# Left blocks of split products read from their first place, and their combinations made in the row buffers

## The chip, the cores and the metric

The kernel runs on one core of one Trainium2 chip. The metric is the device time of one execution in microseconds. The time before is the median of three runs. All profiles are single executions, taken by the hardware profiler.

The core has engines with queues of their own: TensorE (PE in the profile, its weight loads PEld), VectorE (DVE), ScalarE (ACT), GpSimd (POOL) and SyncE (SP). Transfers are issued from the queues of SyncE, ScalarE and GpSimd.

## The reference

Two graph layers over 4096 nodes with 512 features, each with a residual and a layer norm. The second layer is attention over the adjacency matrix:

```python
# layer 0
x = layernorm(x + relu(adj @ (max(sign(x), 0) @ sign(W0).T)))
# layer 1
node_att = softmax(x @ node_w, axis=0)
h = x @ edge_w
e = where(adj > 0, h @ h.T, -9e15)
combined = node_att * softmax(e, axis=1)
out = layernorm(x + (adj * combined) @ (x @ weight) + bias)
```

All data are 32-bit floats. Here only the last large product matters, the aggregation `(adj * combined) @ (x @ weight)`, which the kernel computes as `((adj * combined) @ x) @ weight`, transposed.

## The kernel before

The kernel works in stages: layer 0 (to about 507 us), the projection `h` (to 606), the scores `e` with their row statistics (to about 1086 us), and the aggregation with the final layer norm (to the end). Products are done with seven multiplications for eight (Strassen's scheme in Winograd's form): two operands of 2 x 2 blocks each are combined by additions into seven left and seven right operands, and the seven products are added up.

**The left operands** of the aggregation are seven combinations of blocks of `x` after layer 0. They are made there once and stored in DRAM, `lop_d`, in one piece for each of four groups of rows:

```python
    lop_d = [dram.tile([P, 7, BG, HD], F32, name=f"lop_d{g}") for g in range(HG)]

    lop2_d = [dram.tile([P, len(SPLIT), 7, BG // 2, P], F32, name=f"lop2_d{g}") for g in range(HG)]
...
def left(b, low, high):

    to = lop_d[b // BG][:, :, b % BG, :]
    l11, l21, l12, l22 = low[:, :HD], low[:, HD:], high[:, :HD], high[:, HD:]
    s4, s1, s2, s3 = (sums_l[:, n, :] for n in range(4))
    nc.vector.tensor_sub(s3, l11, l21)
    nc.vector.tensor_add(s1, l22, l21)
    nc.vector.tensor_sub(s2, s1, l11)
    nc.vector.tensor_sub(s4, l12, s2)
    nc.gpsimd.dma_start(to[:, 0, :], l11)
    nc.gpsimd.dma_start(to[:, 1:4:2, :], high.rearrange("p (h f) -> p h f", h=2))
    nc.gpsimd.dma_start(to[:, 2, :], s4)
    nc.gpsimd.dma_start(to[:, 4:, :], sums_l[:, 1:, :])
```

**The aggregation** is 16 blocks, four column groups `g` times four row groups `r`. Each block is seven products `m`. Its right operands are made by VectorE and ScalarE during the block before (L823 to L856: scores shifted, exponential, times adjacency, then four differences); its left operands are loaded from `lop_d[r][:, m]`, 512 KB each, into a pool of four buffers:

```python
    rows = ctx.enter_context(tc.tile_pool(name="rows", bufs=4))
...
    lopp = ctx.enter_context(tc.tile_pool(name="lopp", bufs=4))
```

From the fifth block to the last but one, three of the seven products (`SPLIT = 6, 4, 3`) are themselves split into seven smaller ones. Their seven left blocks (three raw quarters of the left operand, `l11`, `l12` and `l22`, and four combinations, into which `l21` goes too) are made once, while the first column group (`g` = 0) still does these products whole. `order` says in which sequence the products come:

```python
def order(self, two):


    ends = (1, 2) if self.r % 2 else (2, 1)
    if self.last:
        order = 1, 0, 5, 2, 6, 4, 3
    elif two:
        order = ends[0], 6, 5, 4, 0, 3, ends[1]
    else:
        order = ends[0], 0, 4, 6, 5, 3, ends[1]
    for m in order:
        if two and m in SPLIT:
            for ns in ((1, 2), (6,), (0, 5), (3, 4)):
                yield Sums(self, m, ns=ns)
        else:

            more = bool(self.r) and m == order[0]
            keep = self.r < HG - 1 and m == order[-1]
            for h in range(2):
                yield Sums(self, m, h, more, keep)
```

`lefts` runs at the end of a whole product of the first column group. In the order of the program it takes a buffer of the left pool for the combinations, makes them with four VectorE additions, and at the next step stores raw quarters and combinations, seven blocks in all, to `lop2_d` from the scalar queue. `main` runs a block and calls it:

```python
def lefts(self, m, lop):

    (l11, l21), (l12, l22) = [[lop[:, k : k + 2, f : f + P] for f in (0, P)] for k in (0, BG // 2)]
    s = lopp.tile([P, 4, BG // 2, P], F32, name="left2", tag="lop")
    s4, s3, s2, s1 = (s[:, n] for n in range(4))

    tc.keep_in_program_order(nc.vector.tensor_add(s1, l21, l22))
    tc.keep_in_program_order(nc.vector.tensor_sub(s2, s1, l11))
    tc.keep_in_program_order(nc.vector.tensor_sub(s3, l11, l21))
    tc.keep_in_program_order(nc.vector.tensor_sub(s4, l12, s2))
    to = lop2_d[self.r][:, SPLIT.index(m)]
    yield
    nc.scalar.dma_start(to[:, :2].rearrange("p n b f -> p (n b) f"), lop[:, :, :P])
    nc.scalar.dma_start(to[:, 2:6], s)
    nc.scalar.dma_start(to[:, 6], l22)
...
def main(self, between, two):
    uses = deque(u for u in plan if u.unit is self)
    whole = sum(u.work for u in uses)
    halves = (None for m in [u.m for u in uses if u.ns and u.ns[0] == 1] for _ in self.second(m))
    stores = deque()
    past = 0
    while plan and plan[0].unit is self:
        u = plan.popleft()
        u.seed()
        u.multiply()
        evict()
        written.append(u)
        for ahead in list(plan)[:3]:
            ahead.seed()
        past += u.work
        if stores:
            next(stores.popleft(), None)
        if not u.ns:
            next(halves, None)
        if u.end:
            free.append(self.right(u.m))
            if not self.g and u.m in SPLIT:
                stores.append(self.lefts(u.m, lops["lop"]))
                next(stores[0])
        between(past / whole, u.work)
    if stores:
        next(stores.popleft(), None)
```

A product then loads what it needs and multiplies. For a whole product that is one transfer; for a split one two, the first four blocks into one buffer and the last three into another:

```python
def multiply(self):
    r, m = self.unit.r, self.m
    if self.begin and not self.ns:
        lops["lop"] = lopp.tile([P, BG, HD], F32, name="lop")
        nc.sync.dma_start(lops["lop"], lop_d[r][:, m])
    elif self.begin:
        for n, c in (("low", slice(0, 4)), ("high", slice(4, 7))):
            lops[n] = lopp.tile([P, 4, BG // 2, P], F32, name="lop2", tag="lop")
            nc.sync.dma_start(lops[n][:, : c.stop - c.start], lop2_d[r][:, SPLIT.index(m), c])
    if self.ns:
        products = []
        for k, n in enumerate(self.ns):
            at = self.lefts[n]
            lop = lops["high"][:, at - 4] if at > 3 else lops["low"][:, at]
            products.append((self.bank[:, ts(k, W // 2)], lop, self.unit.halves[n], BG // 2))
    else:
        products = [(self.bank, lops["lop"][:, :, ts(self.h, P)], self.unit.right(m), BG)]
    start = not r and self.w == W
    for ps, lop, rop, K in products:
        for k in range(K):
            nc.tensor.matmul(ps, lop[:, k, :], rop[:, k, :], start=start, stop=(k == K - 1), skip_group_check=True)
            start = False
```

Each product of 128 x 512 in 32-bit floats shows as two records of TensorE, so a whole product `m` is 2 halves x 4 matmuls x 2 = 16 records.

**The row buffers** (`rows`, four of 2 KB a partition) hold rows of `x` and other short-lived things in earlier stages. In the aggregation only the finishing step of a column group uses them, for the residual rows:

```python
def load(self, some=range(BG)):
    rows_ = x1_d[self.A * W : (self.A + 1) * W, :]
    if self.last:
        xb = take()
        nc.gpsimd.dma_start(xb, rows_.rearrange("(b p) d -> p b d", p=P))
        self.xbs = [xb[:, i, :] for i in range(BG)]
        return
    for i in some:
        self.xbs[i] = rows.tile([P, D], F32, name="xb1", tag="rows")
        nc.sync.dma_start(self.xbs[i], rows_[ts(i, P), :])
```

The first finishing step follows the fourth block (the last of column group 0). Its loads are in the sync queue, as the left loads are[...].

Of the kernel before, what the change touches and what calls it, by code (L numbers as in the profile page):

```python
# [11 lines left out]
F32 = mybir.dt.float32  # L12
# [6 lines left out]
P = 128  # L19
# [5 lines left out]
SPLIT = 6, 4, 3  # L25
# [4 lines left out]
def kernel(  # L30
# [13 lines left out]
    nc = tc.nc  # L44
# [5 lines left out]
    BG = W // P  # L50
    HB = NB // 2
    HG = NG // 2
# [5 lines left out]
    rows = ctx.enter_context(tc.tile_pool(name="rows", bufs=4))  # L58
    small = ctx.enter_context(tc.tile_pool(name="small", bufs=2))
    dram = ctx.enter_context(tc.tile_pool(name="dram", bufs=1, space=bass.MemoryType.DRAM))  # L60
# [17 lines left out]

    lop_d = [dram.tile([P, 7, BG, HD], F32, name=f"lop_d{g}") for g in range(HG)]

    lop2_d = [dram.tile([P, len(SPLIT), 7, BG // 2, P], F32, name=f"lop2_d{g}") for g in range(HG)]

# [5 lines left out]
    def seven(lop, rop, dests, after):  # L90
# [43 lines left out]
        def m3(ps, q, c11, c12, c21, c22):  # L134
            nc.vector.tensor_add(c12, c12, ps)
            after(q, 1)

        multiply(0, 0, True, m1)
        multiply(1, 5, True, u2)
        multiply(2, 4, True, nothing)  # L140
        multiply(1, 6, False, u3)
        multiply(0, 1, False, m2)
# [16 lines left out]
    with (  # L159
# [184 lines left out]
        with tc.manual_schedule(engines={mybir.EngineType.DVE, mybir.EngineType.Activation}):  # L344
            for n in range(NB):
                b = n // 2 + n % 2 * HB
# [43 lines left out]
        lops = stream.tile([P, 4, HK, HD], F32, name="lops", tag="stream")  # L390
        l11, l12 = we_s[:, :HK, :HD], we_s[:, HK:, :HD]
        l21, l22 = we_s[:, :HK, HD:], we_s[:, HK:, HD:]
        s4, s1, s2, s3 = (lops[:, n] for n in range(4))
# [59 lines left out]
    lopp = ctx.enter_context(tc.tile_pool(name="lopp", bufs=4))  # L453
# [345 lines left out]
    class Aggregate:  # L799
# [149 lines left out]
        def lefts(self, m, lop):  # L949

            (l11, l21), (l12, l22) = [[lop[:, k : k + 2, f : f + P] for f in (0, P)] for k in (0, BG // 2)]
            s = lopp.tile([P, 4, BG // 2, P], F32, name="left2", tag="lop")
            s4, s3, s2, s1 = (s[:, n] for n in range(4))

            tc.keep_in_program_order(nc.vector.tensor_add(s1, l21, l22))
            tc.keep_in_program_order(nc.vector.tensor_sub(s2, s1, l11))
            tc.keep_in_program_order(nc.vector.tensor_sub(s3, l11, l21))
            tc.keep_in_program_order(nc.vector.tensor_sub(s4, l12, s2))
            to = lop2_d[self.r][:, SPLIT.index(m)]
            yield  # L960
            nc.scalar.dma_start(to[:, :2].rearrange("p n b f -> p (n b) f"), lop[:, :, :P])
            nc.scalar.dma_start(to[:, 2:6], s)
            nc.scalar.dma_start(to[:, 6], l22)

        def right(self, m):
            r11, t1, r21, r22 = self.q
# [36 lines left out]
    lops = {}  # L1003
# [5 lines left out]
    class Sums:  # L1009
# [32 lines left out]
# [3 lines that stand above are left out]
                lops["lop"] = lopp.tile([P, BG, HD], F32, name="lop")  # L1045
                nc.sync.dma_start(lops["lop"], lop_d[r][:, m])
            elif self.begin:
                for n, c in (("low", slice(0, 4)), ("high", slice(4, 7))):
                    lops[n] = lopp.tile([P, 4, BG // 2, P], F32, name="lop2", tag="lop")
                    nc.sync.dma_start(lops[n][:, : c.stop - c.start], lop2_d[r][:, SPLIT.index(m), c])  # L1050
            if self.ns:
                products = []
                for k, n in enumerate(self.ns):
# [10 lines that stand above are left out]
            if self.keep:  # L1064
                kept.append(self.bank)
# [371 lines left out]
```

## Time and profile before

| | before |
|---|---|
| time, median of 3 runs | 1962.94 us |
| single runs | 1972.32, 1954.82, 1962.94 us |
| span of the profiled run | 1966.4 us |
| TensorE busy | 98% |
| VectorE busy | 71% |
| ScalarE busy | 52% |
| GpSimd busy | 15% |
| mean granted clock of TensorE | 0.993 |
| moved by transfers | 521.82 MB, 265 GB/s |

A line of the page's groups reads: line of the kernel, engine, operation, output and inputs, shape, count; then busy time in all and the mean of one in ns; then the engine's idle time just before these instructions and what ended most of it. `lop_d` in a group stands for both DRAM tensors of left operands, since numbers in names are left out. The issues of transfers, with size of one and the median time from issue to landing, are these for the stores and loads concerned (from 980 us on):

```profile
lop<-lop_d SPq DMA_DIRECT2D x112, 512.0 KB, 4.8
...
lop<-lop_d SPq DMA_DIRECT2D x33, 384.0 KB, 5.0
...
lop_d<-left ACTq DMA_DIRECT2D x12, 512.0 KB, 5.9
...
lop_d<-lop ACTq DMA_DIRECT2D x12, 256.0 KB, 5.2
...
lop_d<-lop ACTq DMA_DIRECT2D x12, 128.0 KB, 5.1
```

The first line is the 79 whole left operands and the 33 first halves of split ones, the second the 33 other halves. The three stores are those of `lefts`, twelve times each.

The stretches of the four blocks of column group 0, with the busy time of TensorE, its weight loads, VectorE, ScalarE and GpSimd (instructions in brackets), the granted clock, the share of the transfer engines and their rate:

```profile
1086.00:1134.00 48.00, 45.10 (x103) 19.60 (x103) 44.65 (x43) 27.91 (x41) 8.98 (x12) 0.96 0.94 338
1134.00:1180.00 46.00, 46.00 (x108) 20.24 (x107) 28.76 (x22) 26.39 (x27) 3.66 (x5) 1.00 0.79 288
1180.00:1245.00 65.00, 54.45 (x122) 23.71 (x122) 38.43 (x30) 33.14 (x39) 8.30 (x12) 0.92 0.86 306
1245.00:1298.00 53.00, 53.00 (x137) 24.53 (x136) 36.58 (x35) 28.35 (x35) 4.49 (x6) 1.00 0.73 247
```

The first number after the stretch is its length.

### The profile page before, as it was taken

The page shows a single profiled execution, that of the slowest core. Times are in us where ns is not written, and L with a number is a line of the kernel's source. Part 1 is how long each engine was busy: PE and PEld are TensorE (multiplying, and loading weights), DVE is VectorE, ACT ScalarE, POOL GpSimd, SP SyncE. Part 2 cuts the span into 40 slices and gives each one's busy share as a digit, 9 for nine tenths or more (in the row PEclk, how much of TensorE's full clock was granted, in tenths as well). Part 3 has the DMA queues.
Part 4 walks back from the last instruction along what each step waited for, and adds up shares of the span by engine and source line. Part 5 has one row for each costly group of instructions (what it writes and reads, how often), then busy time and mean ns, then how long its engine had stood idle before and what let it go on. Part 6 is the DMA issues. An engine that isn't in the chain of part 4 may idle for free.

```text
span 1966.4 us, 20188 instructions
## 1 busy us (share of the span) xinstructions
PE 1926.4 (98%) x6742; PEld 1206.2 (61%) x6742; DVE 1389.8 (71%) x2062; ACT 1021.8 (52%) x1614; POOL 300.1 (15%) x424
## 2 busy tenths in 40 slices
PE   9999999999999999999999997999999999999998
PEld 6888888888544455444545443456666666666655
DVE  7767666676764576567465866577879977798746
ACT  5433333333203576666667655546767577757731
POOL 0122222222341011111121101011111101111100
PEclk9999999999999999999999998999999999999999
DMA  8888888887475577577697988876778777877731
GB/s 312 296 326 305 299 318 321 293 327 286 143 276 193 188 280 275 202 279 285 224 347 264 321 297 291 295 268 230 261 269 291 270 261 261 293 274 258 279 114 43
DMA packets 153223, 521.82 MB, mean 265 GB/s; under 512 B 15008, under 2 KB 24224, under 8 KB 145440
## 3 DMA queue, kind: packets, MB, share of 16 engines
q1 hardware_dynamic: 63072, 226.39, 33.9%
q0 software_dynamic: 66912, 247.49, 33.9%
q10 hardware_dynamic: 23136, 46.67, 6.6%
q8 instruction: 53, 0.87, 0.2%
q14 instruction: 50, 0.41, 0.1%
HBM read 389.94 MB, written 130.55 MB: 265 GB/s over the span
## 4 chain that ended last, share of the span: by engine, by line
PE 69%; DVE 11%; DMA 9%; issue 8%; ACT 2%; POOL 1%; ACTq 0%; POOLq 0%; DVEq 0%; SPq 0%
PE bank L1062 19%; PE seven L702 13%; PE acc L373 11%; PE acc L374 11%; PE pe L633 5%; PE po L1189 3%; PE pt L603 2%; DMA slot<-s_d 2%; PE seven L101 2%; DMA lop<-lop_d 1%; DVE lent L835 1%; DMA lent<-s_d 1%; DVE over L1125 1%; DMA slot<-in_adj_t_dram 1%; DMA lop_d<-left 1%
## 5 line engine op out<-in xcount | busy, mean ns | idle before, releaser
L1062 PE MATMUL bank<-lent,lop 128*128 128x512 f32 (+1 forms) x1292 | 425.2, 480 | 0.0
L373 PE MATMUL acc<-xw,hi 128*128 128x512 f32 x960 | 376.4, 392 | 0.0
L374 PE MATMUL acc<-xw,lo 128*128 128x512 f32 x960 | 374.2, 390 | 0.0
L1062 PE MATMUL bank<-slot,lop 128*128 128x512 f32 (+1 forms) x896 | 351.0, 540 | 13.4 <-DMA lop<-lop_d 10.5
L1062 PEld LDWEIGHTS bank<-lent,lop 128*128 128x128 f32 x1292 | 245.7, 190 | 154.6 <-issue 133.5
L1062 PEld LDWEIGHTS bank<-slot,lop 128*128 128x128 f32 x896 | 171.2, 192 | 169.4 <-issue 156.4
L363 ACT CAST hi<-at 128x1024 fp32r<-128x1024 f32 x120 | 126.4, 1054 | 203.4 <-PE acc L373 148.4
L365 DVE TENSOR_TENSOR lo<-at,hi 128x1024 fp32r<-128x1024 f32 x120 | 146.9, 1224 | 85.4 <-ACT hi L363 85.4
L374 PEld LDWEIGHTS acc<-xw,lo 128*128 128x128 f32 x960 | 180.3, 188 | 37.0 <-DVE lo L365 0.3
L373 PEld LDWEIGHTS acc<-xw,hi 128*128 128x128 f32 x960 | 180.3, 188 | 36.7
L1071 ACT COPY over<-bank 128x512 f32<-128x512 f32 x200 | 114.6, 582 | 124.5 <-PE bank L1062 109.1
L633 PE MATMUL pe<-hT 128*128 128x512 f32 (+3 forms) x384 | 133.7, 491 | 0.0
L565 DVE CUSTOM_DVE_ANT_0 line<-lent,slot 128x512 f32<-128x512 bf16 x144 | 93.1, 688 | 52.7 <-ACT slot L604 27.9
L574 ACT ACTIVATE line<-line,nmax_c 128x512 f32<-128x512 f32 x160 | 115.0, 726 | 20.9 <-DVE nmax_c L565 20.8
L829 ACT ACTIVATE slot<-slot 128x2048 f32<-128x2048 f32 x40 | 76.6, 1914 | 80.3 <-DMA slot<-in_adj_t_dram 66.6
L823 DVE CUSTOM_DVE_ANT_1 slot<-slot,line 128x2048 f32<-128x2048 f32 x36 | 82.3, 2287 | 31.8 <-DMA slot<-s_d 31.4
L633 PEld LDWEIGHTS pe<-hT 128*128 128x128 f32 x384 | 65.5, 193 | 41.8 <-issue 34.4
L702 PE MATMUL seven<-hT 128*128 128x512 f32 x192 | 89.8, 593 | 0.0
L826 ACT ACTIVATE slot<-slot 128x2048 f32<-128x2048 f32 x36 | 68.9, 1915 | 37.8 <-DVE slot L823 37.6
L603 PEld LDWEIGHTS pt<-ident,lent 128*128 128x128 f32 x412 | 51.8, 143 | 59.5 <-issue 39.7
L823 DVE CUSTOM_DVE_ANT_1 lent<-lent,line 128x2048 f32<-128x2048 f32 x28 | 64.0, 2285 | 33.7 <-DMA lent<-s_d 23.9
L604 ACT COPY slot<-pt 128x512 f32<-128x512 f32 (+3 forms) x126 | 69.7, 556 | 31.7 <-PE pt L603 21.7
(260 smaller groups left out, 2886.8 us busy)
## 6 DMA issues: line engine op xcount, KB each, us to landing
at<-in_adj_t_dram SPq DMA_DIRECT2D x60, 1024.0 KB, 6.7
lop<-lop_d SPq DMA_DIRECT2D x112, 512.0 KB, 4.8
slot<-in_adj_t_dram POOLq DMA_DIRECT2D x42, 1024.0 KB, 6.6
slot<-s_d POOLq DMA_DIRECT2D x36, 1024.0 KB, 7.9
s_d<-slot POOLq DMA_DIRECT2D x33, 1024.0 KB, 6.8
lent<-s_d POOLq DMA_DIRECT2D x28, 1024.0 KB, 7.7
lent<-in_adj_dram SPq DMA_DIRECT2D x48, 512.0 KB, 5.3
s_d<-lent POOLq DMA_DIRECT2D x48, 512.0 KB, 4.2
```

The lines of the kernel that those rows point to most:

```text
L363: nc.scalar.copy(hi, aq)
L365: nc.vector.tensor_sub(lo, aq, hi.bitcast(F32))
L373: nc.tensor.matmul(acc, hi[:, c, :], xw[:, kb, :], start=(kb == 0), stop=False)
L374: nc.tensor.matmul(acc, lo[:, c, :], xw[:, kb, :], start=False, stop=(kb == NB - 1))
L565: nc.vector.tensor_tensor_reduce(line, mask, src, -1.0, HUGE, ALU.add, ALU.min, accum_out=nmax_c[:, b, c : c + 1])
L574: nc.scalar.activation(line, line, AF.Exp, bias=nmax_c[:, b, c : c + 1], scale=-1.0, accum_out=sum_c[:, b, c : c + 1])
L603: nc.tensor.transpose(pt[:, j, :], src[:, ts(j, P)], ident)
L633: nc.tensor.matmul(pe[:, lo * P :], hT[:, k, ts(A * BG + i, P)], hT[:, k, (B * BG + lo) * P : (B + 1) * W], start=(k == 0), stop=(k == KD ...
L702: nc.tensor.matmul(ps, left[m][:, k, q, :], right[m][:, k, :], start=(first and k == 0), stop=(k == KD // 2 - 1), skip_group_check=not first,)
L823: pinned[0](nc.vector._custom_dve(TENSOR_ADD_SAT, out=q, in0=q, in1=m, s0=0.0, s1=-HUGE))
L1062: nc.tensor.matmul(ps, lop[:, k, :], rop[:, k, :], start=start, stop=(k == K - 1), skip_group_check=True)
L1071: nc.scalar.copy(self.to(), self.bank[:, : self.w])
```

## The change

The raw quarters are no longer copied to the second DRAM tensor; split products load them from `lop_d`, where they lie within the whole left operand. Only the four combinations are stored. And the combinations are made in two row buffers in place of one buffer of the left pool, so that the left pool holds left operands alone. A split product now has four loads for its two buffers: two raw quarters (256 KB, runs of 512 bytes), two combinations (256 KB), two combinations (256 KB), a raw quarter (128 KB, runs of 512 bytes).

The order in which things are issued shifts with it, since the framework places instructions by the buffers they wait for. TensorE's order differs in one place of the first block (the fourth product's first four records stand ahead of the third product's), VectorE's in the places of some operations within the first six blocks, and the first four loads of residual rows, which stood ahead of all left loads in the sync queue, now stand behind the left loads of the first column group and ahead of the first split product's.

```diff
--- before.py
+++ after.py
@@ -78,7 +78,7 @@
 
     lop_d = [dram.tile([P, 7, BG, HD], F32, name=f"lop_d{g}") for g in range(HG)]
 
-    lop2_d = [dram.tile([P, len(SPLIT), 7, BG // 2, P], F32, name=f"lop2_d{g}") for g in range(HG)]
+    lop2_d = [dram.tile([P, len(SPLIT), 4, BG // 2, P], F32, name=f"lop2_d{g}") for g in range(HG)]
 
 
 
@@ -949,8 +949,8 @@
         def lefts(self, m, lop):
 
             (l11, l21), (l12, l22) = [[lop[:, k : k + 2, f : f + P] for f in (0, P)] for k in (0, BG // 2)]
-            s = lopp.tile([P, 4, BG // 2, P], F32, name="left2", tag="lop")
-            s4, s3, s2, s1 = (s[:, n] for n in range(4))
+            s = [rows.tile([P, 2, BG // 2, P], F32, name="left2", tag="rows") for _ in range(2)]
+            s4, s3, s2, s1 = (x[:, n] for x in s for n in range(2))
 
             tc.keep_in_program_order(nc.vector.tensor_add(s1, l21, l22))
             tc.keep_in_program_order(nc.vector.tensor_sub(s2, s1, l11))
@@ -958,9 +958,8 @@
             tc.keep_in_program_order(nc.vector.tensor_sub(s4, l12, s2))
             to = lop2_d[self.r][:, SPLIT.index(m)]
             yield
-            nc.scalar.dma_start(to[:, :2].rearrange("p n b f -> p (n b) f"), lop[:, :, :P])
-            nc.scalar.dma_start(to[:, 2:6], s)
-            nc.scalar.dma_start(to[:, 6], l22)
+            for n in range(2):
+                nc.scalar.dma_start(to[:, ts(n, 2)], s[n])
 
         def right(self, m):
             r11, t1, r21, r22 = self.q
@@ -1045,9 +1044,13 @@
                 lops["lop"] = lopp.tile([P, BG, HD], F32, name="lop")
                 nc.sync.dma_start(lops["lop"], lop_d[r][:, m])
             elif self.begin:
-                for n, c in (("low", slice(0, 4)), ("high", slice(4, 7))):
-                    lops[n] = lopp.tile([P, 4, BG // 2, P], F32, name="lop2", tag="lop")
-                    nc.sync.dma_start(lops[n][:, : c.stop - c.start], lop2_d[r][:, SPLIT.index(m), c])
+                low, high = (lopp.tile([P, 4, BG // 2, P], F32, name="lop2", tag="lop") for _ in range(2))
+                raw, s = lop_d[r][:, m], lop2_d[r][:, SPLIT.index(m)]
+                nc.sync.dma_start(low[:, :2].rearrange("p n b f -> p (n b) f"), raw[:, :, :P])
+                nc.sync.dma_start(low[:, 2:], s[:, :2])
+                nc.sync.dma_start(high[:, :2], s[:, 2:])
+                nc.sync.dma_start(high[:, 2], raw[:, BG // 2 :, P:])
+                lops["low"], lops["high"] = low, high
             if self.ns:
                 products = []
                 for k, n in enumerate(self.ns):
```

## The prediction

> **What bounds the kernel now.** I read the page's busy times first, then what TensorE waits for, then its timeline around those waits, and last the chain of work and the waits of the queue that issues the loads.
>
> ```profile
> PE 1926.4 (98%) x6742; PEld 1206.2 (61%) x6742; DVE 1389.8 (71%) x2062; ACT 1021.8 (52%) x1614; POOL 300.1 (15%) x424
> ...
> L1062 PE MATMUL bank<-slot,lop 128*128 128x512 f32 (+1 forms) x896 | 351.0, 540 | 13.4 <-DMA lop<-lop_d 10.5
> ```
>
> TensorE is busy 98% of the span, 40 us of 1966.4 are not. The product line L1062, the one the change feeds, is idle for 13.4 us in all, and 10.5 of them end with the arrival of a left operand. The waits of TensorE (us in total, times, longest) say how that splits:
>
> ```profile
> PE bank L1062 <- DMA lop<-lop_d: 10.5, 1, 10.5
> PE po L1189 <- DVE xb L1200: 7.0, 7, 2.6
> PE pt L603 <- ACT slot L604: 4.7, 1, 4.7
> PE bank L1062 <- DVE slot L850: 2.8, 1, 2.8
> ```
>
> So it is one stall of 10.5 us, not many small ones. Its place, in the timeline of TensorE (start, duration, with the idle time in brackets):
>
> ```profile
> 1093.36 7.03 PE L1062 MATMUL bank<-slot,lop 128*128 128x512 f32 x16
> 1103.23 8.83 PE L1062 MATMUL bank<-slot,lop 128*128 128x512 f32 x16 [2.85 <-DVE slot L850]
> ...
> 1180.68 7.03 PE L1062 MATMUL bank<-slot,lop 128*128 128x512 f32 x16
> 1198.25 9.15 PE L1062 MATMUL bank<-slot,lop 128*128 128x512 f32 x16 [10.55 <-DMA lop<-lop_d]
> 1207.24 27.63 PE L1062 MATMUL bank<-lent,lop 128*128 128x512 f32 x64
> ```
>
> One product is 16 records and occupies 6.87 us (1153.21 to 1160.08 in this timeline, start to start). The first aggregation block runs from 1086.1, the second from 1139.4 for seven products, so the third could start at 1187.7. It starts at 1198.25, and its first product takes 9.15 us instead of 7.03. The chain of waits says why:
>
> ```profile
> 1174.82 1.94 issue
> 1176.76 2.29 DVE slot L835
> 1179.04 0.34 DVE left L955
> 1179.38 2.20 DVE lent L848
> 1181.58 0.34 DVE left L956
> 1181.91 0.34 DVE left L957
> 1182.25 0.34 DVE left L958
> 1182.60 0.02 issue
> 1182.62 8.02 DMA lop_d<-left
> 1190.70 7.42 DMA lop<-lop_d
> 1198.25 53.78 PE bank L1062 x120
> ```
>
> VectorE reaches the four combinations of the second block's last split product only at 1179 to 1182.6, their store takes 8.02 us, and only then may the next left operand be loaded, 7.42 us. The store is between them because the combinations lie in one of the four left buffers. The load queue confirms it:
>
> ```profile
> SPq L1046 <- DMA lop_d<-left: 85.3, 8, 23.2
> SPq L1050 <- DMA lop_d<-left: 10.5, 1, 10.5
> ```
>
> Eight left loads waited for such a store, the longest 23.2 us; one of them wasn't hidden. After 1198.25 TensorE waits only for the last finishing products (7.0 us).
>
> **What the Trainium skill says.** "Perfetto Trace Analysis", Identifying the Most-Contended Engine, says that gaps on the engine that should be saturated can mean that no SBUF buffer is free for the next tile. That fits: the missing thing is a buffer. "DMA: Bandwidth & Descriptors", Anatomy of one DMA, puts a fixed cost of about 2 us on each transfer, independent of size; the trace agrees, a 128 KB store of this kernel lands in 2.3 us at best, but the median under load is 5.1, so four transfers for two matter only if they are late. The same page, Specifications, asks for 512 bytes or more for line rate; the new raw loads have runs of exactly 512 bytes. The store of the same raw blocks in the kernel before has such runs too, and its 256 KB land in 5.2 us at the median, against 5.9 for the 512 KB of combinations, so no penalty is seen. "TensorE: Matmul & The Clock Gate", Why this matters for your kernels, warns of a lower clock after idle gaps over about 3 us. The trace agrees: 9.15 us after the 10.55 us gap, 2.12 more than 7.03, and 8.83 after a gap of only 2.85, 1.80 more.
>
> **The change, part by part.** *The combinations leave the left buffers.* A first-pass block loads 7 left operands and makes 3 sets of combinations, so it took 10 of the rotating left buffers and now takes 7. The first load of the third block then reuses the buffer four products earlier, the fourth of block two. TensorE is through with that at 1139.4 + 4 x 6.87 = 1166.9, VectorE has read it by 1163.8. A load at 1167 with 7.4 us to land is there at 1174.5, 13 us before 1187.7. The 10.55 us go, and with the gap its slow first product, 2.12 us: 12.7 us.
>
> Would another operand stop TensorE at 1187.7 instead? Its right block comes from the product at 1176.76, which ends at 1179.05; the differences for the third to sixth products end between 1181.6 and 1191.7, and are wanted at 1201 and later. So no.
>
> *The first block.* The fourth left operand no longer shares the rotation with a set of combinations, so it can be loaded before the block starts. In the order of instructions of the changed kernel the fourth product's first half-group (4 records) now stands ahead of the third product. The fourth's right block is ready at 1098.56 + 2.29 = 1100.85, the third's at 1100.89 + 2.29 = 1103.18, and TensorE is free at 1100.39. At 6.87 / 16 = 0.43 us a record, 4 x 0.43 = 1.7 us of work fit in the gap of 2.85; with some of the slow clock I count 2 us.
>
> *Stores.* Three of seven blocks are no longer copied: 3 x 128 KB in each of 12 sets, 4.7 MB. In the four first-pass blocks the windows give 62 MB (338, 288, 306 and 247 GB/s over 48, 46, 65 and 53 us), so 7.6% less in the stretch in which the queues are fullest. It gives latency, not time on the path. The scalar queue issues 12 x 3 = 36 stores before and 24 after, 0.34 to 0.37 us each, 4 us of an engine that is 52% busy: nothing.
>
> *Loads.* 33 split products load the same bytes in four transfers for two: 66 more issues at 0.32 us, 21 us on the sync queue, which mostly waits. A split product's second half is issued when the split product before it is 8/14 through, and wanted some 12.5 us later (2.6 of its rest, 6.9 of the whole product between, 3.0 of the first half); the landing is 4.6 us at the median, 8.0 at most in the split loads. Two more issues of 0.32 fit. Cost on the path: 0.
>
> *Row buffers.* They serve the residual rows of the finishing step too. The first four of these loads used to be issued before 986 us and now come after the last set's store, in front of the first split product's loads, in the same in-order queue. Before, that store was issued at 1288.96 and had landed when the split load followed at 1295.62; the split product wanted it at 1305.16, with 4.6 us to land that left 5. Now up to four issues stand ahead, and one raw part: about 1.5 us. Some 3 us of slack stay, if TensorE and VectorE move forward together. VectorE's idle time of 15.3 us ahead of 1252.96, where it waits for TensorE, says that they do. I allow 1.5 us for this place or a like one.
>
> The sum: 12.7 + 2 - 1.5 = 13 us, 0.67%: 1962.9 - 13 = 1950.
>
> **The rivals.** *VectorE takes over as the wait.* For it: 71% busy over the span, and 44.65 of 48 us in the first block. If it were ahead by less than 12.7 us, the next block would give back what the third won. Against it: after 1237.7 it stands idle until TensorE reaches the panel, 15.3 us. Under this rival the gain is 2 to 6 us, 1957 to 1961. *The load queue becomes the wait.* For it: four transfers for each split product, 512-byte runs, and the row loads stand in the same queue (one such pair held a second half back from 1361.75 to 1372.29 without a wait on TensorE). With 2 us lost in a third of the 33 split products it would cost 22 us: about 1972. Against it: the slack of 7 us worked out above. *The stall is one run's accident.* It is made of an 8.02 and a 7.42 us transfer, both slower than the medians of 5.9 and 4.8; at the medians it would be 5.8 us instead of 10.5. Then the timed runs win some 8 us, 1955.
>
> **Range and chances.** Single runs of the kernel before spread over 17.5 us (1954.82 to 1972.32), so medians of a few runs can be off by 5 or so each. I say 1950 us, and 1938 to 1963 eight times in ten. Over 2% either way means 39 us; the whole idle time of TensorE is 40, so faster by that gets 0.02, slower 0.03, and within 2% 0.95.
>
> **What would show it right or wrong.** Right: no wait of the product line for a left load, the third block's first product at 1188 less the 2 us of the first block, 7.0 us long, and no load that waits for a store of combinations. The load queue's waits should be on TensorE. Wrong: a new wait of TensorE near the first split product (about 1290) or at split products for a left load; a wait on a right block in the third or fourth block; or a gain that is there at the fourth block's end and gone at the end of the span.

## The result, and the profile after

| | before | after |
|---|---|---|
| time, median | 1961.83 us (4 runs) | 1943.06 us (4 runs) |
| single runs | 1954.82 to 1972.32 | 1939.64 to 1944.82 |
| ratio | | 0.9898, 95% interval 0.9851 to 0.9945 |
| span of the profiled run | 1966.4 us | 1940.4 us |

The change takes 18.8 us off, 1.0%; 13 were predicted. The interval of the ratio reaches from 11 to 29 us, so these times alone don't tell the two apart. A second comparison, on other executions (at the end of the experiments), gives 16.7 us. The profiled run of before is one of its slower ones, so its span differs by more (26 us) than the medians do.

The page of the changed kernel, busy times and the groups of the product line, which is now L1065 (idle time before them at the end):

```profile
PE 1918.7 (99%) x6742; PEld 1203.0 (62%) x6742; DVE 1389.6 (72%) x2062; ACT 1022.4 (53%) x1614; POOL 299.5 (15%) x424
...
L1065 PE MATMUL bank<-lent,lop 128*128 128x512 f32 (+1 forms) x1292 | 424.6, 479 | 0.7 <-issue 0.7
...
L1065 PE MATMUL bank<-slot,lop 128*128 128x512 f32 (+1 forms) x896 | 347.0, 535 | 0.3 <-DVE slot L850 0.3
```

VectorE and ScalarE do the same work as before to within a microsecond. TensorE's product line is idle for 1.0 us where it was 13.4, and no left load ends any of it. The waits of TensorE (us, times, longest):

```profile
PE po L1192 <- DVE xb L1203: 3.8, 6, 1.3
PE pt L603 <- DVE lent L747: 2.2, 1, 2.2
```

Two waits of before are missing here that the prediction treated differently: the left load (10.5 us), and the 4.7 us on ScalarE (slot L604), to which the prediction gave no part. TensorE's timeline in the places shown before:

```profile
1089.07 7.03 PE L1065 MATMUL bank<-slot,lop 128*128 128x512 f32 x16
1096.84 1.95 PE L1065 MATMUL bank<-lent,lop 128*128 128x512 f32 x4 [0.73 <-issue]
1099.11 7.13 PE L1065 MATMUL bank<-slot,lop 128*128 128x512 f32 x16 [0.32 <-DVE slot L850]
...
1173.03 13.90 PE L1065 MATMUL bank<-slot,lop 128*128 128x512 f32 x32
1186.77 27.63 PE L1065 MATMUL bank<-lent,lop 128*128 128x512 f32 x64
```

The four early records fill most of the first block's gap. The second block's last product and the third block's first are now one group of 32 records without a gap. The load queue's waits show what the left loads depend on:

```profile
SPq L1045 <- PE bank L1065: 346.2, 68, 8.3
...
SPq L1045 <- DVE left L958: 22.1, 3, 8.7
...
SPq L1157 <- DMA lop_d<-left: 7.5, 2, 6.8
```

Whole left operands wait for TensorE and, three times, for VectorE's last combination; the only loads that wait for a store of combinations are the first residual rows (L1157).

To see where the time went, I read three marks from each profile's timeline of TensorE: the start of the aggregation (first record of the product line), and the starts of its second, third and fourth block. A block without a wait takes 48.1 us. The last column is from the fourth block's start to the end of the span.

| kernel | aggregation starts | block 1 | block 2 | block 3 | three blocks | the rest |
|---|---|---|---|---|---|---|
| before | 1086.1 | 53.3 | 58.9 | 50.2 | 162.3 | 718.0 |
| before, second profile | 1084.5 | 55.0 | 52.0 | 50.6 | 157.7 | 715.8 |
| after | 1081.8 | 50.0 | 48.1 | 48.1 | 146.2 | 712.4 |
| after, second profile | 1080.2 | 49.7 | 48.1 | 48.1 | 145.8 | 713.2 |
| combinations in row buffers only | 1088.1 | 50.6 | 48.1 | 48.1 | 146.7 | 714.4 |
| raw blocks from their place only | 1079.1 | 52.4 | 49.6 | 48.1 | 150.2 | 713.1 |
| raw stores held late | 1079.0 | 56.4 | 51.5 | 51.0 | 158.9 | 714.6 |
| the same, second profile | 1080.8 | 56.0 | 55.3 | 50.2 | 161.5 | 717.6 |
| row buffers, raw stores held late | 1081.3 | 50.3 | 48.1 | 50.1 | 148.5 | 715.8 |
| after, raw stores put back | 1088.0 | 50.7 | 48.1 | 48.1 | 146.8 | 714.3 |
| after, a left buffer taken again | 1080.0 | 51.5 | 48.1 | 48.1 | 147.6 | 712.4 |
| after, differences of the last weights held late | 1079.6 | 49.0 | 48.1 | 48.1 | 145.1 | 714.1 |

The second profiles of before and after are of executions within 2 us of their medians (1959.7 us beside 1961.4, 1941.1 beside 1943.1). Between them the start gains 4.2 us, the three blocks 11.9, the rest 2.6: 18.7 in all. Two thirds are the left loads and the first block, as predicted; the other third isn't in the prediction.

The start is gained in the score stage. ScalarE of the kernel before near 1012 us (`ACTq` is its queue issuing a transfer):

```profile
1005.39 0.59 ACT L744 COPY lent<-seven 128x512 f32<-128x512 f32 x1 [1.11 <-PE seven L702]
1014.36 0.39 ACTq L961 DMA_DIRECT2D lop_d<-lop  x1
1014.78 1.04 ACTq L963 DMA_DIRECT2D lop_d<-lop  x1
1015.87 0.59 ACT L604 COPY slot<-pt 128x512 f32<-128x512 f32 x1 [9.90 <-issue]
```

The raw stores of the first set stand in the scalar queue in the score stage, 93 us before the combinations of that set are made. They wait for a left load, which was issued at 1001.9 us and took 12.3 us to land, until 1014.3; the copies behind them in the queue wait too: 9.90 us idle, which the profile puts down to "issue". TensorE then runs out of emptied banks:

```profile
1010.36 1.46 PE L633 MATMUL pe<-hT 128*128 128x384 f32 x4
1016.51 1.11 PE L603 MATMUL pt<-ident,lent 128*128 128x128 f32 x4 [4.70 <-ACT slot L604]
```

In the changed kernel there are no raw stores, and ScalarE goes on in the same place:

```profile
1007.01 0.59 ACT L744 COPY lent<-seven 128x512 f32<-128x512 f32 x1 [1.12 <-PE seven L702]
1010.02 0.59 ACT L604 COPY slot<-pt 128x512 f32<-128x512 f32 x1 [2.43 <-PE pt L603]
```

The copy L744 of these two views is the last of its line in every profile, and stands ahead of the raw stores. Counted from it, the aggregation starts 80.7 and 79.4 us later in the two profiles of before, 83.3 and 84.3 us later in two kernels below that have two sets of raw stores there, and 73.8 to 75.9 us later in all eight profiles that have none. This comparison leaves out what differs between executions in earlier stages (the copy itself comes anywhere from 1003.7 to 1007.0).

### The profile page after: what moved, and what is told of

Same layout as the page of the kernel before. It is cut to its first block, busy times and chain, and to the rows that moved or that the text cites. A ratio compares the mean times of both kernels' runs of the same rounds, so it can differ in the third digit from the quotient of the medians.

```text
span 1940.4 us, 20257 instructions
## 1 busy us (share of the span) xinstructions
PE 1918.7 (99%) x6742; PEld 1203.0 (62%) x6742; DVE 1389.6 (72%) x2062; ACT 1022.4 (53%) x1614; POOL 299.5 (15%) x424
## 4 chain that ended last, share of the span: by engine, by line
PE 76%; DVE 10%; issue 6%; DMA 6%; ACT 1%; POOL 1%; POOLq 0%; DVEq 0%; SPq 0%; ACTq 0%
PE bank L1065 25%; PE seven L702 12%; PE acc L374 11%; PE acc L373 11%; PE pe L633 4%; PE seven L101 4%; PE po L1192 3%; PE pt L603 2%; DMA s_d<-slot 2%; DMA slot<-s_d 2%; DVE lent L835 1%; PE acc L246 1%; PE pw L214 1%; PE pt L333 1%; DVE over L1128 1%
## 5 line engine op out<-in xcount | busy, mean ns | idle before, releaser
L1065 PE MATMUL bank<-lent,lop 128*128 128x512 f32 (+1 forms) x1292 | 424.6, 479 | 0.7 <-issue 0.7
L1065 PE MATMUL bank<-slot,lop 128*128 128x512 f32 (+1 forms) x896 | 347.0, 535 | 0.3 <-DVE slot L850 0.3
L1065 PEld LDWEIGHTS bank<-lent,lop 128*128 128x128 f32 x1292 | 245.2, 190 | 155.0 <-issue 133.6
L1065 PEld LDWEIGHTS bank<-slot,lop 128*128 128x128 f32 x896 | 170.0, 190 | 153.4 <-issue 142.3
L829 ACT ACTIVATE slot<-slot 128x2048 f32<-128x2048 f32 x40 | 76.5, 1913 | 73.8 <-DMA slot<-in_adj_t_dram 64.7
L1037 ACT COPY bank<-over 128x512 f32<-128x512 f32 x144 | 84.8, 596 | 2.9 <-DVE left L957 0.2
L603 PEld LDWEIGHTS pt<-ident,lent 128*128 128x128 f32 x412 | 51.1, 141 | 55.1 <-issue 40.0
L604 ACT COPY slot<-pt 128x512 f32<-128x512 f32 (+3 forms) x126 | 69.5, 555 | 27.8 <-PE pt L603 24.0
```

The costliest lines, as they stand in the source:

```text
L603: nc.tensor.transpose(pt[:, j, :], src[:, ts(j, P)], ident)
L1037: nc.scalar.copy(self.bank[:, : self.w], self.to())
```

## The experiments

The theory with which I went to the chip: two in-order queues. Left loads are held by a store that sits in the left pool, and ScalarE is held in the score stage by raw stores that wait for a left load. Rival A: the score stage gained because the residual rows' loads left the sync queue, where they waited 23.8 us in front of mask loads. Rival B: fewer bytes to store shorten all waits. Each ratio below is to runs of the kernel before made beside it; its medians in the three groups of runs are 1961.54, 1963.16 and 1959.82 us.

**Each part of the change alone.** Combinations in the row buffers, raw blocks still copied:

```diff
-            s = lopp.tile([P, 4, BG // 2, P], F32, name="left2", tag="lop")
+            s = [rows.tile([P, 2, BG // 2, P], F32, name="left2", tag="rows") for _ in range(2)]
...
-            nc.scalar.dma_start(to[:, 2:6], s)
+            for n in range(2):
+                nc.scalar.dma_start(to[:, ts(n + 1, 2)], s[n])
```

> Combinations in the row buffers, everything else as in the kernel before (raw blocks still copied, two loads for a split product). Theory (two in-order queues: left loads held by a store that sits in the left pool, 10.5 us and 2.1 us of slow clock after it, and ScalarE held by raw stores that wait for a left load, 4.7 us of TensorE wait near 1012 us and about 1 us of slow clock): the wait of the product line for a left load is gone, the first block is 3 us shorter, but the wait of TensorE on ScalarE near 1012 us stays or grows, because the raw stores are still there (now two sets of them stand in the score stage). 1946 to 1951. Rival A (the score stage gained because the row loads left the sync queue, where they waited 23.8 us ahead of mask loads): that wait is gone here too, 1941. Rival B (4.7 MB less to store is what shortens the waits): the left load is still waited for, 5 us or more, 1955 or above.

Measured 1949.3 us, ratio 0.9926 (0.9900 to 0.9951): 12 us. No wait for a left load, the three blocks in 146.7 us. The score stage is slower than before (83.3 us from the copy L744), against rival A: the row loads have left the front of the sync queue here too. ScalarE shows two sets of raw stores now, and that the second waits for a left load by name:

```profile
1013.73 0.39 ACTq L961 DMA_DIRECT2D lop_d<-lop  x1
1014.15 0.71 ACTq L964 DMA_DIRECT2D lop_d<-lop  x1
1014.90 0.58 ACT L604 COPY slot<-pt 128x512 f32<-128x512 f32 x1 [9.44 <-issue]
...
1019.14 0.37 ACTq L961 DMA_DIRECT2D lop_d<-lop  x1
1019.61 1.15 ACT L574 ACTIVATE lent<-lent,nmax_c 128x1024 f32<-128x1024 f32 x1 [4.12 <-DMA lop<-lop_d]
```

Raw blocks from their own place, combinations still in a left buffer:

```diff
-            s = [rows.tile([P, 2, BG // 2, P], F32, name="left2", tag="rows") for _ in range(2)]
-            s4, s3, s2, s1 = (x[:, n] for x in s for n in range(2))
+            s = lopp.tile([P, 4, BG // 2, P], F32, name="left2", tag="lop")
+            s4, s3, s2, s1 = (s[:, n] for n in range(4))
...
-            for n in range(2):
-                nc.scalar.dma_start(to[:, ts(n, 2)], s[n])
+            nc.scalar.dma_start(to, s)
```

(against the changed kernel)

> Raw blocks from their own place (four loads for a split product, only combinations stored), combinations still in a buffer of the left pool. Theory: the wait on ScalarE near 1012 us is gone (no raw stores), the product line's wait for a left load stays, 5 to 11 us, the first block keeps its gap of 2.85: 1956. Rival A: row loads are as early as before, so the wait near 1012 us stays: 1962. Rival B: the store of combinations lands so much earlier that the wait for the left load is gone or below 3 us: 1948.

Measured 1947.85 us, ratio 0.9913 (0.9887 to 0.9940): 14 us, where the theory gave 6. The score stage is free, as the theory had it, with the row loads as early as before, so rival A is out from this side too. But the wait for the left load is nearly gone as well:

```profile
1172.68 7.03 PE L1064 MATMUL bank<-slot,lop 128*128 128x512 f32 x16
1181.12 7.11 PE L1064 MATMUL bank<-slot,lop 128*128 128x512 f32 x16 [1.41 <-DMA lop<-lop_d]
```

Its chain of waits is the same as before, with shorter links:

```profile
1168.72 0.43 DVE left L958
1169.15 0.02 issue
1169.17 5.83 DMA lop_d<-left
1175.01 0.02 SPq L1044
1175.03 0.03 issue
1175.06 5.92 DMA lop<-lop_d
```

Rival B of this run is what was measured, in the time and in the wait. What the raw stores have to do with this wait is less clear. Against the first profile of before the wait is 9.1 us shorter: counted from the second block's start (1131.5, before 1139.4), the store goes out at 37.7 us instead of 43.2, and store and load together land 3.7 us sooner. But in the second profile of before, raw stores included, the same store goes out at 37.4 us, so the earlier issue isn't shown to come from their absence. There the store lands in 8.14 us, the load in 6.28, and TensorE waits 3.78:

```profile
1191.53 7.10 PE L1062 MATMUL bank<-slot,lop 128*128 128x512 f32 x16 [3.78 <-DMA lop<-lop_d]
```

So 2.4 us of that wait are gone, through the faster landing of store and load, in one profile, which is of the fastest of the four runs (1944.09 us). The score stage accounts for 5.5 to 6.9 of the 13.7 us; the raw stores cost something in the aggregation too, and by what way isn't shown by this run. The two parts alone give 12.2 and 13.7 us, both together 18.8 or 16.7: they overlap by 7 to 9. In the first three blocks, against the second profile of before, the parts alone gain 11.0 and 7.5 us and both together 11.9, so most of the overlap is there.

**The raw stores by themselves.** The kernel before, with its raw stores held at their place of the program:

```diff
-            nc.scalar.dma_start(to[:, :2].rearrange("p n b f -> p (n b) f"), lop[:, :, :P])
+            tc.keep_in_program_order(nc.scalar.dma_start(to[:, :2].rearrange("p n b f -> p (n b) f"), lop[:, :, :P]))
...
-            nc.scalar.dma_start(to[:, 6], l22)
+            tc.keep_in_program_order(nc.scalar.dma_start(to[:, 6], l22))
```

> The kernel before with one thing changed: the raw stores are held at their place of the program in the scalar queue, behind the first block's copies, instead of standing in the score stage. Theory: TensorE's wait of 4.7 us on ScalarE near 1012 us is gone, with its slow clock 6 us; the wait for the left load stays, 5 to 12 us: 1956. Rival A (row loads): nothing gained, the wait stays, 1962.

Measured 1961.32 us, ratio 1.0000 (0.9988 to 1.0013): nothing gained. Yet the score stage's wait is gone, and the aggregation starts at 1079.0. So the expectation was wrong in the whole while right in the place. A second profile was to tell where it goes:

> The same kernel as the one with pinned raw stores, for a second profile, since the first is of the fastest of its 20 executions (1954.3 against a median of 1961.3). Theory: the aggregation starts near 1079 us, 5 us earlier than before, and what is won is lost again in TensorE's waits for left loads in the first three blocks, which then take 160 to 166 us instead of 158 to 162. Rival: the start isn't earlier, or the time is lost after the fourth block.

Measured 1962.62 us, ratio 1.0001 (0.9987 to 1.0016). Start at 1080.8, the three blocks in 161.5:

```profile
1116.09 7.10 PE L1062 MATMUL bank<-lent,lop 128*128 128x512 f32 x16 [2.90 <-DMA lop<-lop_d]
...
1192.08 9.17 PE L1062 MATMUL bank<-slot,lop 128*128 128x512 f32 x16 [7.08 <-DMA lop<-lop_d]
```

and in the load queue of the same profile

```profile
SPq L1046 <- DMA lop_d<-left: 87.6, 8, 22.8
...
SPq L1046 <- DMA lop_d<-lop: 64.1, 11, 11.8
```

Before, left loads waited 7.5 us for raw stores (`lop_d<-lop`), here 64.1. A late raw store holds the left buffer that it reads until it has landed. Against the second profile of before the start gains 3.7 us, the three blocks lose 3.8 and the rest 1.8; against the first one the blocks lose nothing (161.5 and 162.3). The first of these profiles, of an execution at 1954.3 us, shows the loss less clearly (158.9 us), so that the gain is given back in the first three blocks rests on one pair of profiles, and on the next kernel.

Raw stores held late, with the combinations in the row buffers:

```diff
-            s = lopp.tile([P, 4, BG // 2, P], F32, name="left2", tag="lop")
+            s = [rows.tile([P, 2, BG // 2, P], F32, name="left2", tag="rows") for _ in range(2)]
```

(with the stores as in the first experiment, and the raw ones held as in the one above)

> Combinations in the row buffers, raw blocks still copied, but their stores held at their place of the program in the scalar queue. Theory as revised (the raw stores cost twice: early in the scalar queue they hold ScalarE in the score stage; late, they hold the left buffers they read until they have landed): no wait on ScalarE near 1012 us, the aggregation starts about 5 us earlier than with the stores early, but the left loads wait for raw stores, so that some us of TensorE's waits for left loads come in the first three blocks: 1945 to 1949. Rival (the queue place alone matters, the buffers are held harmlessly once the combinations are out of the pool): 1943, with the first three blocks in 146 us as in the changed kernel.

Measured 1946.45 us, ratio 0.9909 (0.9881 to 0.9937). The start is early (1081.3), and one wait for a left load is back:

```profile
PE bank L1063 <- DMA lop<-lop_d: 1.8, 1, 1.8
```

Left loads wait 130.3 us for raw stores here, 16.5 with the raw stores early. The wait is what the theory as revised foresaw; its single runs scatter from 1941.76 to 1953.61, so the time alone would not tell it from its rival.

**The loads, and the buffer.** The changed kernel with the raw stores put back, read by nobody:

```diff
+            nc.scalar.dma_start(to[:, 4:6].rearrange("p n b f -> p (n b) f"), lop[:, :, :P])
             for n in range(2):
                 nc.scalar.dma_start(to[:, ts(n, 2)], s[n])
+            nc.scalar.dma_start(to[:, 6], l22)
```

> The changed kernel with the raw stores put back into the scalar queue, into a place that nobody reads; split products keep their four loads. It differs from the kernel with combinations in the row buffers alone (1949.3) only in the loads. Theory: four loads and 512-byte runs cost nothing: 1948 to 1951. Rival: the loads cost, and the changed kernel wins in spite of them: 1953 or above.

Measured 1951.66 us, ratio 0.9945 (0.9924 to 0.9966), 0.7 us over the upper end of what the theory gave. Its table row is the same as that of the row buffers alone to within 0.2 us in every column, and their intervals overlap: four loads in place of two cost nothing that shows. The raw stores' price is seen once more: start at 1088.0.

The changed kernel with a left buffer taken for each set, one column written into it, nothing stored from it:

```diff
+            idle = lopp.tile([P, 4, BG // 2, P], F32, name="idle2", tag="lop")
+            tc.keep_in_program_order(nc.vector.tensor_copy(idle[:, 0, 0, 0:1], s4[:, 0, 0:1]))
```

> The changed kernel, with a buffer of the left pool taken for each set of combinations again, but only one column written into it by VectorE and nothing stored from it. So the turn of the buffers is as before, and no buffer waits for a store. Theory (what costs is that the buffer is held until its store has landed, about 8 us): 1 to 4 us slower than the changed kernel, 1944 to 1947, with a wait of at most 3 us for a left load. Rival (the missing turn alone costs): a wait of 5 us or more for a left load, 1950.

Measured 1941.89 us, ratio 0.9894 (0.9874 to 0.9914): as fast as the changed kernel, not the 1 to 4 us slower that the theory gave. Left loads wait 77.7 us for VectorE's one column, and none of it reaches TensorE; only the first block is 1.5 to 1.8 us longer, since the fourth product's early records are missing again. So the turn in the pool is free. What costs is a buffer that isn't released before its store has landed.

**For comparison and for more.** The kernel before, unchanged:

> The kernel before, unchanged, for a second profile. Theory: both waits of TensorE are there again (on ScalarE near 1012 us, on a left load at the third block's start), each differing by some us from the first profile, since both end with the landing of a transfer. Rival: one or both are an accident of the first profile and are missing.

Measured 1961.41 us. Both waits are there: 4.4 us on ScalarE, and for left loads 6.1 us in two pieces (3.8 at the third block, 2.3 at the fourth) where the first profile had 10.5 in one.

The changed kernel, and one thing more that its profile offered: the four differences of the last weights stand in front of the first block's last right operands. Held at their place in the program instead:

```diff
-            todo.append(lambda: nc.vector.tensor_sub(t3, r22, r12))
+            todo.append(lambda: tc.keep_in_program_order(nc.vector.tensor_sub(t3, r22, r12)))
```

(and the three after it alike)

> The changed kernel with one thing more: the four VectorE differences of the last weights (lines L1367 to L1370) are held at their place in the program, in the second block, where they stood ahead of the first block's last right operands (4 us with the wait for the weights' load). The first block's third and fourth product are then there 4 us earlier, and TensorE's gaps of 0.73 and 0.32 us with the slow clock behind them should go: the first block 48.1 to 48.6 us instead of 50.0. Theory: 1.5 to 2 us faster than the changed kernel. Rival: VectorE gives the 4 us back in the second block and delays the combinations or right operands there: no gain.

> The changed kernel again, for comparison on the same chip, and for a second profile: no wait for a left load; 1943.

Measured 1942.06 us with it, ratio 0.9899 (0.9871 to 0.9927), and 1943.12 without, 0.9906 (0.9878 to 0.9935). The first block takes 49.0 us instead of 49.7, not the 48.1 to 48.6 expected: the gap of 0.73 us is gone, that of 0.32 is still 0.29. The second and third block are unchanged, against the rival, and the rest is longer (714.1 us beside 713.2), with a new wait of 0.8 us at 1692.9 for a bank that ScalarE fills. A gain isn't shown.

## Why the prediction was right or wrong

*The combinations leave the left buffers, 12.7 us: right, and of the right size for the profile it was read from.* The second and third block took 58.9 and 50.2 us there and take 48.1 and 48.1, 12.9 less. Its argument "the store is between them because the combinations lie in one of the four left buffers" holds: with the store gone from the pool (row buffers alone) the wait is gone, and a buffer without a store does no harm. But the third rival, "the stall is one run's accident", was half right: the second profile has 52.0 and 50.6, 6.5 us to win. So for a typical execution this term was about twice too large.

*The first block, 2 us: right in kind, too small.* 53.3 and 55.0 us before, 50.0 and 49.7 after: 3.3 and 5.4 us. The early records themselves are worth 1.5 to 1.8, by the run with a left buffer taken again, which lacks them. The other part is mostly the slow clock behind the gap: 16 records took 8.83 and 9.80 us before (granted clock 0.81 and 0.72), and 7.13 us in that run, at 1.00, though its gap is 2.46 us long.

*Stores: this step failed.* It counted 12 issues fewer on the scalar queue, "4 us of an engine that is 52% busy: nothing", and for the bytes "latency, not time on the path". The runs show two costs of the raw stores. In the scalar queue of the score stage they hold ScalarE by 9 to 10 us and TensorE by 4 to 5, and the way from the copy L744 to the aggregation is 3.5 to 6.9 us longer than in the profiles without them there. I counted how long an issue takes and not how long it waits for its data with the queue behind it. The place was in the waits of TensorE that I showed, "PE pt L603 <- ACT slot L604: 4.7", and I didn't ask what ScalarE was waiting for. And raw blocks from their own place alone bring 13.7 us, more than the score stage gives, so "not time on the path" fails in the aggregation too. By what way the early raw stores cost there isn't shown; late ones hold left buffers, and left loads wait 61.6 to 130.3 us for them.

*Loads, cost 0: right.* The kernel with raw stores put back shows it: 1951.66 us beside 1949.3, with overlapping intervals and the same table row. In the changed kernel the four loads of a split product landed, in the order of their issue, in 3.4, 4.2, 5.1 and 5.4 us at the median, the first and the last being the raw ones; kind and place in the order go together here, so these medians don't compare the lengths of runs. "DMA: Bandwidth & Descriptors" in the Trainium skill (Specifications) asks for 512 bytes or more for line rate, and nothing here speaks against it. The fixed 2 us that the prediction takes from that page are given there for transfers issued from GpSimd; for the ones here the quickest landings are 2.3 us for a store of 128 KB and 2.8 us for a load of 256 KB.

*Row buffers, 1.5 us allowed: not needed.* The first split product's four loads went out between 1267.4 and 1272.6 us, and it began at 1284.69. The last of them, issued at 1271.52, took 6.0 us to land: 7.1 us ahead, not the 3 of the prediction. The stores had landed earlier, and VectorE moved forward with TensorE, as argued.

*Not foreseen: 2.6 us of the rest* (5.6 in the first pair of profiles). It begins at the first finishing step: TensorE reaches the product record 264 places behind the fourth block's start 4.8 and 3.6 us sooner, and in the second pair gives 1 us back later. Before, three loads were held behind VectorE and went out together, and the last one, issued at 1311.98 us, took 12.02 us to land by the chain of waits (the timeline of GpSimd's queue in the kernel before):

```profile
1310.50 0.75 POOL L817 DMA_DIRECT2D slot<-in_adj_t_dram  x1 [11.00 <-DVE d L789]
1311.24 0.75 POOL L810 DMA_DIRECT2D slot<-s_d  x1
1311.98 0.75 POOL L810 DMA_DIRECT2D lent<-s_d  x1
```

The profile names VectorE's panel sum (L789), but most of the 11 us were over before it: the chain has the queue waiting for a multiplication (L835) until 1309.96, and for the panel sum only 0.5 us more.

```profile
1307.75 2.21 DVE lent L835
1309.96 0.03 POOLq L817
1309.99 0.49 issue
```

In the changed kernel the loads are spread over the time from 1278 to 1298:

```profile
1291.19 0.75 POOL L810 DMA_DIRECT2D lent<-s_d  x1 [5.30 <-PE bank L1065]
1298.06 0.75 POOL L817 DMA_DIRECT2D lent<-in_adj_t_dram  x1 [6.12 <-PE bank L1065]
```

The panel sum has the same place in VectorE's order there; the multiplication stands five places earlier. Counted from the fourth block's start, the held load goes out at 62.1 and 61.8 us in the profiles of before, at 48.2 in both of the changed kernel, at 49.9 and 48.2 with either part alone, and at 60.6 to 62.1 in the three profiles with raw stores held late. So either part of the change frees it, and late raw stores bring it back. That the order of VectorE is the cause was read from the traces and tried by no run. The prediction noted the moved operations and gave them no number.

The rivals *VectorE takes over* and *the load queue becomes the wait* are out: after the third block's start no product waits on either. Two of the prediction's signs came out a little differently: the third block starts at 1179.9 us, not at about 1186, since the score stage and the first block give more; and two loads do still wait for a store of combinations, the residual rows (7.5 us), without a wait of TensorE.

That 13 lies near what was measured is in part luck. In the sum of the second pair of profiles the left loads give 6.5 us where 12.7 stood, and the first block 5.4 where 2 stood; the 1.5 us allowed for the row buffers weren't needed; and 4.2 us of the start and 2.6 of the rest were in no term.

## What to carry to other kernels

A transfer issued from a compute engine's queue waits for its data in that queue, so look in the order of instructions for where it stands, not only for what an issue costs: here a store placed 93 us early held ScalarE for 9.9 us. A buffer is as long in use as the slowest thing that reads it; the stores of combinations here took 2.6 to 11.8 us to land (in the kernel before), the product that reads a left operand takes 7. So results that are to be stored belong outside the pool that feeds the engine to be kept busy, and data that already lie in DRAM need not be stored from it again. When one profile offers a single long wait, take a second one before putting a size on it.

## What the runs showed of the hardware

Four transfers in place of two for the same bytes, a part of them in runs of 512 bytes, cost no time that shows (1951.66 us beside 1949.3, with overlapping intervals). Transfers that wait for their data in ScalarE's queue held its copies for 9.44 to 9.90 us in the four profiles that have such transfers early. The slow clock behind a gap varies: after 2.85 us of gap 16 records took 8.83 us (granted clock 0.81) and after 3.27 us 9.99 (0.71), but after 3.78 us 7.10, at a clock of 1.00. So the limit of about 3 us that the prediction takes from the Trainium skill isn't a sharp one here: the clock fell behind a shorter gap and stayed up behind a longer one.
